# Other planning figures for dealing expert parts over the places of a scan, in a fused scan and mixture-of-experts kernel

## The chip, the cores and the metric

The kernel runs on one core of one Trainium2 chip. Five engines work side by side, each taking its own instructions in order: TensorE (PE in the profile, with its weight loads as PEld), VectorE (DVE), ScalarE (ACT), GpSimd (POOL) and SyncE (SP, which here only issues DMAs). The metric is the device time of one execution in microseconds (us), as the median of several runs. The profile is one further execution, recorded instruction by instruction.

## The reference

The input x is 2 x 2048 tokens of 256 numbers, in float32. It is normalised (layer norm), and two things are added to it:

```
xn  = layernorm(x)
# 1: every token gets a cluster (argmax of cosine with 8 means); tokens are sorted by cluster;
#    over the sorted tokens runs a selective scan, for 256 channels and 16 states each:
h_t = exp(delta_t * A) * h_(t-1) + (delta_t * u_t) * B_t        # per channel and state
y_t = sum over the states of h_t * C_t  +  D * u_t
#    and y is put back in the order of the tokens
# 2: a mixture of experts: 8 experts, each token takes its best 2
h   = silu(xn @ w1[e]) * (xn @ w3[e])                            # 256 -> 512
out = sum over the 2 experts of prob * (h @ w2[e])               # 512 -> 256
x   = x + y + out
```

## The kernel before

**The front** (up to about 100 us) loads x, computes statistics, scores and routes, and lists which tokens go to which expert. After that two streams of work are woven together.

**The scan stream.** The tokens are cut into 8 pieces of 512 (2 batches x 4). Each piece has 8 steps: 4 groups of 4 states, times 2 halves of the channels. So there are 64 steps, and each step has 4 places (one per state), which makes 256 places, numbered 0 to 255 here. At every place VectorE does one multiply (`feed`, L840, for the next place) and one scan (`scan`, L849), and ScalarE makes the decay of the place four further on (`decay`, L834). TensorE works on the step before: at the second place of a step (places 1, 5, 9, ...) it transposes blocks 0 and 1 of the finished states, at the third place blocks 2 and 3 (`Step.turn`, L861), and at the fourth place it contracts them with C (`contract`, L870). ScalarE copies each transposed block out of PSUM (L865); the transposes have two PSUM buffers (`ps_t`), so blocks 2 and 3 need the copies of blocks 0 and 1. In what follows T01, T23 and C stand for these three blocks of TensorE work.

**The expert stream.** Rows are grouped into 71 tiles of 128 rows of one expert; 68 tiles are dealt, the last 3 stand behind a condition at the end. A tile has three parts: up 0 and up 1 (`up`, L954, 16 matmuls each, 256 to 512) and down (`down`, L977, 8 matmuls, 512 to 256). With an up 0 goes a tanh on ScalarE (L962) and a multiply on VectorE (`silu`, L967); with an up 1 the multiply `gate` (L971). These two multiplies are not issued with the part but two places later (`later`, L1044), or when a next part needs them (`vector_work`, L1035). The up parts have one PSUM buffer each. A down part first turns the rows of the tile after next (`turn_tile`, L1059: two transposes L937, a ScalarE copy L939 and two tiny VectorE operations L941, L945), then does its matmuls, a scaling copy on ScalarE (L981), and issues on GpSimd's queue the next rows, the addition to the output (L895) and the next weights (L914). Up 0 of tile 24 is written U0-24 here, its up 1 U1-24, its down D24.

**Who sets the order.** The order of all instructions is written out by a loop at build time (L1159 to L1195) and kept on every engine (`keep_order`). The list `jobs` holds 204 parts in a fixed order: U0-0, U1-0, U0-1, U1-1, D0, U0-2, U1-2, D1, and so on. 7 of them come ahead of the scans; the loop deals the other 197 over the places. Each place has a planned load for TensorE (`on_pe`) and for VectorE (`on_dve`), in us; other work of the pieces is entered with `at_place` (transposes of inputs, projections, step sizes `size`, masks, starting sums `begin`). After each place the loop deals parts as long as the planned TensorE time so far, plus half a part, is under `ratio` times the planned VectorE time so far. `ratio` is planned TensorE time over planned VectorE time of the whole. Before, every part counts 2.05 for TensorE and 0.5 for VectorE:

```
        on_dve[n] += 1.75
            on_pe[n] += (0.0, 0.9, 0.9, 1.1)[n % NSUB]
    PART, PART_DVE = 2.05, 0.5
                pe_now + PART / 2 < ratio * dve_now or place + 1 >= n_places
```

The step sizes of a next piece (`size`, with eight ScalarE operations L732) are held back until the next down part is due (`behind_down`, `size_now`, L1107).

**Within a place** the text order is: feed and scan; T01, T23 or C of the step before; a decay; what `at_place` put there; the parts dealt there; the multiplies that are due.

Of the kernel before, what the change touches and what calls it, by code (L numbers as in the profile page):

```python
# [56 lines left out]
def scan_moe_kernel(  # L57
# [968 lines left out]
    NSUB = Q  # L1026
# [8 lines left out]
    def vector_work(t: int):  # L1035

        for when in sorted(later):
            later[when] = [(u, do) for u, do in later[when] if u > t or do()]

    def part_up(t: int, i: int):  # L1040
        def do():
            vector_work(t - 1)
            tiles[t].up(i)
            later.setdefault(now + 2, []).append((t, tiles[t].silu if i == 0 else tiles[t].gate))  # L1044
            if i == 1 and t + NW < n_dealt:
                tiles[t + NW].load_up()
        return do

    def part_down(t: int):
        def do():  # L1050
            if t + 2 < n_dealt:
                turn_tile(t + 2)
            vector_work(t)
            tiles[t].down()
            if t + NW < n_dealt:
                tiles[t + NW].load_down()
        return do

    def turn_tile(t: int):  # L1059
        tiles[t].turn()  # L1060
        if t + NW < n_dealt:
            tiles[t + NW].load_rows()
# [4 lines left out]
    jobs = []  # L1067
    for t in range(n_dealt + 1):
        if t < n_dealt:
            jobs += [part_up(t, 0), part_up(t, 1)]  # L1070
        if t > 0:
            jobs.append(part_down(t - 1))
    turn_tile(0)
    turn_tile(1)
    p = pieces[0]
# [8 lines left out]
    ahead = len(lead)  # L1084
# [10 lines left out]
    given = ahead  # L1095
    n_places = NSUB * (len(steps) - 1)
# [6 lines left out]
    on_pe, on_dve = [0.0] * n_all, [0.0] * n_all  # L1103
# [3 lines left out]
    def size_now():  # L1107
        while behind_down and (given % 3 == 2 or given == len(jobs)):
            behind_down.pop(0)()
# [39 lines left out]
        at_place(2 * q - 1, 2, lambda q=q: pieces[0].mask_z(q), 0.0, 0.6)  # L1149

    for n in range(NSUB * len(steps)):
        on_dve[n] += 1.75
        if n >= NSUB:
            on_pe[n] += (0.0, 0.9, 0.9, 1.1)[n % NSUB]
    PART, PART_DVE = 2.05, 0.5
    left = len(jobs) - ahead
    ratio = (sum(on_pe[:n_places]) + left * PART) / (sum(on_dve[:n_places]) + left * PART_DVE)
    pe_now = dve_now = 0.0
    for k in range(len(steps)):  # L1159
        step = steps[k]  # L1160
        before_ = steps[k - 1] if k else None
        for i in range(NSUB):
            if i + 1 < NSUB:
                step.feed(i + 1)
            elif k + 1 < len(steps):
                steps[k + 1].feed(0)
            step.scan(i)
            if before_:
                if i == 0:
                    before_.keep_last()  # L1170
                elif i < 3:
                    before_.turn(2 * i - 2)
                    before_.turn(2 * i - 1)
                else:
                    for n in range(JC):
                        before_.contract(n)
            if k + 1 < len(steps):
                steps[k + 1].decay(i)
            for do in plan.pop((k, i), []):
                do()  # L1180
            size_now()
            place = k * NSUB + i
            pe_now += on_pe[place]
            dve_now += on_dve[place]
            while given < len(jobs) and (
                pe_now + PART / 2 < ratio * dve_now or place + 1 >= n_places
            ):
                jobs[given]()
                given += 1
                pe_now += PART  # L1190
                dve_now += PART_DVE
                size_now()
            for _, do in later.pop(now, []):
                do()
            now += 1  # L1195
# [86 lines left out]
```

## Time and profile before

| | us |
|---|---|
| median of 3 runs | 751.91 (751.2 to 751.93) |
| the profiled execution, its own time | 752.28 |
| its span, first to last instruction | 750.5 |
| PE busy | 678.0 |
| PEld busy | 588.9 |
| DVE busy | 678.5 |
| ACT busy | 508.0 |
| POOL busy | 523.0 |
| first scan starts (place 0) | 99.86 |
| last scan ends (place 255) | 735.2 |

The mean granted TensorE clock is 0.951 of full speed, nearly all of the rest in the front. In lines of the timeline the columns are start, duration, engine, source line, operation, what is written and read, count, and in brackets the idle time of the engine just ahead and what ended it. In lines of the waits they are: who waited, at which line, for whom, the total in us, how often, the longest. A matmul's end is modelled in the profile; so the time that a block of matmuls takes on TensorE is read here from its start to the start of the next block.

### The profile page before, as it was taken

To read this page: it belongs to the slowest core of one execution; us is meant where nothing else is said; L and a number is where in the kernel's file an instruction comes from. 1 tells how busy PE (TensorE), PEld (TensorE's weight loads), DVE (VectorE), ACT (ScalarE), POOL (GpSimd) and SP (SyncE) were. 2 spreads that over 40 slices of the span, in tenths; PEclk is the share of its full clock that TensorE was granted. 3 is DMA by queue.
4 is the path that set the end of the run, shared out by engine and by line. 5 is a ranking of instruction groups with operands and counts; after the bars stand their busy time and mean duration, and the time that the engine had idled before them with its cause. 6 is when DMAs were issued, how large, how long until landed. Compare 5 with 4: busy or idle time off the path is not lost.

```text
span 750.5 us, 16877 instructions
## 1 busy us (share of the span) xinstructions
PE 678.0 (90%) x6506; PEld 588.9 (78%) x6506; DVE 678.5 (90%) x1085; ACT 508.0 (68%) x983; POOL 523.0 (70%) x362
## 2 busy tenths in 40 slices
PE   7375779999998999999999999999999998999993
PEld 5144678888877998888878898999798977899982
DVE  8885389899987999999999999999999997999991
ACT  4830446686758866886769577967795768767762
POOL 2023448667777788777877887788788888887733
PEclk9755979999999999999999999999999999999996
DMA  8676544584436755685458656865575547745312
GB/s 269 243 162 233 166 162 92 159 244 138 124 56 171 252 146 117 171 264 148 114 132 281 160 130 124 255 198 132 119 249 157 128 93 219 227 125 118 86 17 29
DMA packets 60401, 120.31 MB, mean 160 GB/s; under 512 B 24160, under 2 KB 41248, under 8 KB 53152
## 3 DMA queue, kind: packets, MB, share of 16 engines
q0 software_dynamic: 38784, 63.71, 36.0%
q1 hardware_dynamic: 21536, 55.50, 21.9%
q8 instruction: 52, 0.85, 0.5%
q14 instruction: 29, 0.24, 0.1%
HBM read 170.78 MB, written 22.28 MB: 257 GB/s over the span
## 4 chain that ended last, share of the span: by engine, by line
PE 69%; ACT 11%; DVE 9%; DMA 5%; issue 4%; POOL 1%; POOLq 0%; ACTq 0%; DVEq 0%
PE p_ps L954 29%; PE py L977 13%; PE pt_s L861 11%; PE y L870 7%; DMA w<-in_w_down_dram,w_row 3%; ACT ht L865 3%; PE y L796 2%; PE pl L342 2%; PE pt_g L937 2%; DMA out_dram<-yo,token_of 2%; ACT da L834 2%; DVE st L374 1%; ACT e L732 1%; ACT r L732 1%; PE px L667 1%
## 5 line engine op out<-in xcount | busy, mean ns | idle before, releaser
L954 PE MATMUL p_ps<-xT,w 128*128 128x128 f32 x2176 | 272.6, 281 | 12.3 <-DVE g L971 8.1
L954 PEld LDWEIGHTS p_ps<-xT,w 128*128 128x128 f32 x2176 | 258.0, 195 | 26.3 <-DVE g L971 8.3
L849 DVE TENSOR_TENSOR_SCAN hs<-da,carry,bu 128x512 f32<-128x512 f32 x192 | 246.0, 1281 | 0.0
L834 ACT ACTIVATE da<-dl,na 128x512 f32<-128x512 f32 x256 | 183.7, 734 | 0.2 <-DVE dl L789 0.2
L840 DVE TENSOR_TENSOR bu<-du,bt 128x512 f32<-128x512 f32 x256 | 173.1, 676 | 0.0
L865 ACT COPY ht<-pt_s 128x512 f32<-128x512 f32 x256 | 138.4, 595 | 40.3 <-PE pt_s L861 39.3
L895 POOL DMA_INDIRECT out_dram<-yo,token_of x68 | 131.4, 1932 | 48.0 <-ACT yo L981 22.6
L914 POOL DMA_INDIRECT w<-in_w_up_dram,w_row x68 | 91.8, 1350 | 89.2 <-DVE w_row L595 43.4
L861 PE MATMUL pt_s<-ident,hs 128*128 128x128 f32 x1024 | 136.8, 277 | 9.7 <-ACT ht L865 8.6
L977 PE MATMUL py<-w,g 128*128 128x256 f32 x544 | 129.8, 381 | 7.5 <-ACT xT L939 4.8
L861 PEld LDWEIGHTS pt_s<-ident,hs 128*128 128x128 f32 x1024 | 116.5, 142 | 21.4 <-ACT ht L865 13.4
L977 PEld LDWEIGHTS py<-w,g 128*128 128x128 f32 x544 | 98.0, 190 | 20.6 <-ACT xT L939 6.0
L928 POOL DMA_INDIRECT xg_sb<-xn,token_of x68 | 91.8, 1349 | 26.2 <-issue 12.8
L914 POOL DMA_INDIRECT w<-in_w_down_dram,w_row x68 | 94.7, 1392 | 20.7 <-issue 13.4
L895 POOL DMA_INDIRECT out_dram<-yt,line_of x32 | 66.1, 2065 | 23.0 <-issue 11.3
L849 DVE TENSOR_TENSOR_SCAN hs<-da,bu 128x512 f32<-128x512 f32 x64 | 78.1, 1221 | 0.0
L962 ACT ACTIVATE t_sb<-p_ps 128x512 f32<-128x512 f32 x68 | 41.0, 603 | 54.5 <-PE p_ps L954 54.4
L870 PE MATMUL y<-ht,z 128*32 128x128 f32 x2048 | 74.0, 277 | 1.5 <-PEq L1208 0.7
L981 ACT ACTIVATE yo<-py,own 128x256 f32<-128x256 f32 x68 | 32.3, 475 | 61.4 <-PE py L977 58.8
L967 DVE SCALAR_TENSOR_TENSOR t_sb<-t_sb,p_ps 128x512 f32<-128x512 f32 x68 | 45.8, 674 | 26.1 <-ACT t_sb L962 26.1
L870 PEld LDWEIGHTS y<-ht,z 128*32 128x32 f32 x2048 | 50.8, 109 | 19.6 <-issue 10.2
L632 POOL DMA_INDIRECT xs<-xn,line_of x32 | 41.8, 1306 | 14.7 <-issue 8.2
(202 smaller groups left out, 582.0 us busy)
## 6 DMA issues: line engine op xcount, KB each, us to landing
bt<-bc SPq DMA_DIRECT2D x31, 1024.0 KB, 5.1
z<-bc SPq DMA_DIRECT2D x32, 256.0 KB, 3.2
xn<-xt SPq DMA_DIRECT2D x8, 520.0 KB, 2.6
xt<-in_x_dram SPq DMA_DIRECT2D x8, 512.0 KB, 8.0
out_dram<-in_x_dram SPq DMA_DIRECT2D x8, 512.0 KB, 8.3
w<-in_w_up_dram,w_row POOLq DMA_INDIRECT x68
w<-in_w_down_dram,w_row POOLq DMA_INDIRECT x68
xg_sb<-xn,token_of POOLq DMA_INDIRECT x68
```

What stands on the lines that cost most here:

```text
L834: nc.scalar.activation(self.da[i], self.piece.dl[:, self.h, :], AF.Exp, scale=na[:, self.h, n : n + 1])
L840: nc.vector.tensor_mul(self.bu[i], self.piece.du[:, self.h, :], self.piece.bts[self.q][:, i, :])
L849: nc.vector.tensor_tensor_scan(self.hs[:, :, i], self.da[i], self.bu[i], start, ALU.mult, ALU.add)
L861: nc.tensor.transpose(pt[:, j, :], self.hs[:, t0 : t0 + G, :].rearrange("p t n -> p (t n)"), ident)
L865: nc.scalar.copy(self.ht[i], pt)
L870: nc.tensor.matmul(p.ys[self.h][j * G : (j + 1) * G, i, :], lhsT=p.zs[q][:, i * (P // G) + j, :], rhs=self.ht[i][:, j, :], start=False, st ...
L895: ins = nc.gpsimd.indirect_dma_start(out=out_rows, out_offset=bass.IndirectOffsetOnAxis(ap=numbers, axis=0), in_=rows, in_offset=None, com ...
L914: nc.gpsimd.indirect_dma_start(out=to[self.t % NW], out_offset=None, in_=rows, in_offset=bass.IndirectOffsetOnAxis(ap=w_row[:, self.t : se ...
L928: nc.gpsimd.indirect_dma_start(out=self.xg, out_offset=None, in_=xn_d, in_offset=bass.IndirectOffsetOnAxis(ap=token_of[:, self.t : self.t ...
L954: nc.tensor.matmul(p[:, f, :], lhsT=wk[:, h, f * P : (f + 1) * P], rhs=self.xT[:, h, :], start=h == 0, stop=h == ND - 1,)
L967: nc.vector.scalar_tensor_tensor(self.s, self.s, 1.0, self.p1, ALU.add, ALU.mult)
L977: nc.tensor.matmul(py, lhsT=self.g[:, f, :], rhs=w2[:, f, :], start=f == 0, stop=f == NH - 1)
```

## The change

The planning figures are replaced, and nothing else: no instruction is added or taken away, and every engine's work is the same.

```diff
--- before.py
+++ after.py
@@ -1070,6 +1070,9 @@
             jobs += [part_up(t, 0), part_up(t, 1)]
         if t > 0:
             jobs.append(part_down(t - 1))
+
+    UP, DOWN, GATE, OWN = 2.0, 2.4, 0.67, 0.36
+    job_pe = [DOWN if n % 3 == 1 and n > 1 else UP for n in range(len(jobs))]
     turn_tile(0)
     turn_tile(1)
     p = pieces[0]
@@ -1149,12 +1152,12 @@
         at_place(2 * q - 1, 2, lambda q=q: pieces[0].mask_z(q), 0.0, 0.6)
 
     for n in range(NSUB * len(steps)):
-        on_dve[n] += 1.75
+        on_dve[n] += 1.95
         if n >= NSUB:
-            on_pe[n] += (0.0, 0.9, 0.9, 1.1)[n % NSUB]
-    PART, PART_DVE = 2.05, 0.5
-    left = len(jobs) - ahead
-    ratio = (sum(on_pe[:n_places]) + left * PART) / (sum(on_dve[:n_places]) + left * PART_DVE)
+            on_pe[n] += (0.0, 1.07, 1.07, 1.14)[n % NSUB]
+    left = sum(job_pe[ahead:])
+    left_dve = (len(jobs) - ahead) * (2 * GATE + OWN) / 3
+    ratio = (sum(on_pe[:n_places]) + left) / (sum(on_dve[:n_places]) + left_dve)
     pe_now = dve_now = 0.0
     for k in range(len(steps)):
         step = steps[k]
@@ -1183,12 +1186,12 @@
             pe_now += on_pe[place]
             dve_now += on_dve[place]
             while given < len(jobs) and (
-                pe_now + PART / 2 < ratio * dve_now or place + 1 >= n_places
+                pe_now + job_pe[given] / 2 < ratio * dve_now or place + 1 >= n_places
             ):
                 jobs[given]()
+                pe_now += job_pe[given]
+                dve_now += (2 * GATE + OWN) / 3
                 given += 1
-                pe_now += PART
-                dve_now += PART_DVE
                 size_now()
             for _, do in later.pop(now, []):
                 do()
```

An up part now counts 2.0 and a down part 2.4 for TensorE; for VectorE each part counts (2 x 0.67 + 0.36) / 3 = 0.57. The scan's own load at each place is entered higher too: VectorE 1.95, TensorE 1.07, 1.07 and 1.14. The sums of the plan become: TensorE 244.7 + 420.4 = 665.1 (before 221.2 + 403.8 = 625.0), VectorE 548.9 + 111.6 = 660.5 (before 498.5 + 98.5 = 597.0), so `ratio` goes from 1.047 to 1.007.

Worked through by the loop's own arithmetic with the one and the other set, 175 of the 197 dealt parts keep their place, and 22 change it, none by more than two places:

| later by one place | later by two | earlier by one |
|---|---|---|
| U0-13 (33 to 34), U1-20 (62 to 63), D27 (95 to 96), U0-30 (101 to 102), U1-35 (122 to 123), D35 (126 to 127), U1-38 (135 to 136), D43 (157 to 158), U0-50 (182 to 183), U0-52 (187 to 188), D51 (188 to 189), D52 (192 to 193), U0-54 (193 to 194), D53 (198 to 199), U0-65 (238 to 239), U0-66 (242 to 243) | U0-46 (162 to 164) | D2 (3 to 2), D4 (10 to 9), U1-16 (52 to 51), U1-18 (57 to 56), U1-40 (145 to 144) |

The order of the parts among themselves stays, and the step sizes of every piece keep their places (14, 48, 80, 111, 142, 174, 208).

## Prediction

> **What bounds the kernel now.** The page first. Both big engines stand at 90%, so shares decide nothing:
>
> ```profile
> PE 678.0 (90%) x6506; PEld 588.9 (78%) x6506; DVE 678.5 (90%) x1085; ACT 508.0 (68%) x983; POOL 523.0 (70%) x362
> ...
> PE 69%; ACT 11%; DVE 9%; DMA 5%; issue 4%; POOL 1%; POOLq 0%; ACTq 0%; DVEq 0%
> ```
>
> The chain that ended last lies on PE for 69%. Who waits for whom settles it. First VectorE's waits from 110 us to the end of the scans, then TensorE's from 110 to 637:
>
> ```profile
> DVE t_sb L967 <- ACT t_sb L962: 18.5, 11, 4.4
> ```
>
> ```profile
> PE pt_s L861 <- ACT ht L865: 8.1, 15, 2.2
> PE py L977 <- ACT xT L939: 4.8, 5, 1.4
> PE p_ps L954 <- ACT xT L939: 2.8, 4, 1.1
> ```
>
> VectorE waits 18.5 us in 11 places, each time for a tanh behind an up 0 that TensorE did late. TensorE's list has no wait for VectorE; it waits for ScalarE copies of its own results. So up to VectorE's last wait TensorE, with ScalarE's copies in it, sets the pace, and VectorE is tied to it again at each wait: places 46 (3.26 us), 52 (4.43), 83 (1.32), 114 (2.05), 177 (0.84), 207 (1.61) and 212, the last:
>
> ```profile
> 631.79 0.16 DVE L945 TENSOR_TENSOR own<-own,xg_sb 128x1 f32<-128x1 f32 x1
> 635.77 0.69 DVE L967 SCALAR_TENSOR_TENSOR t_sb<-t_sb,p_ps 128x512 f32<-128x512 f32 x1 [3.82 <-ACT t_sb L962]
> 636.38 0.68 DVE L840 TENSOR_TENSOR bu<-du,bt 128x512 f32<-128x512 f32 x1
> ```
>
> From 636 VectorE runs without a wait to the last scan (735.2), and 15.3 us of tail follow. The span is therefore: when TensorE reaches U0-57 at place 212 (632.3, tanh done 635.74), plus a stretch set by VectorE. After place 212 only U0-65 and U0-66 move, where their multiplies had 1.0 and 1.15 us to spare; VectorE's operations there stay the same. What counts is how long TensorE takes to get to U0-57.
>
> **What a block costs, by what stands beside it.** The same blocks in TensorE's timeline in two surroundings:
>
> ```profile
> 345.43 2.02 PE L954 MATMUL p_ps<-xT,w 128*128 128x128 f32 x16
> 347.29 1.04 PE L861 MATMUL pt_s<-ident,hs 128*128 128x128 f32 x8
> 348.62 1.15 PE L861 MATMUL pt_s<-ident,hs 128*128 128x128 f32 x8 [0.29 <-ACT ht L865]
> 349.60 1.95 PE L954 MATMUL p_ps<-xT,w 128*128 128x128 f32 x16
> 351.48 1.08 PE L870 MATMUL y<-ht,z 128*32 128x128 f32 x32
> 352.49 0.44 PE L937 MATMUL pt_g<-ident,xg_sb 128*128 128x128 f32 x2
> ```
>
> ```profile
> 504.74 1.04 PE L861 MATMUL pt_s<-ident,hs 128*128 128x128 f32 x8
> 505.71 1.28 PE L870 MATMUL y<-ht,z 128*32 128x128 f32 x32
> 506.92 1.27 PE L954 MATMUL p_ps<-xT,w 128*128 128x128 f32 x9
> ```
>
> Start to start. T01 with T23 right behind takes 347.29 to 348.62, 1.33 (it waits for copies), and that T23 0.98; with a part between each takes 0.87. No part between T01 and T23 costs 0.57. C right behind T23 takes 1.21 (505.71 to 506.92) and T23 before it 0.97; with a part between, C takes 1.01 (351.48 to 352.49), T23 0.87. An up takes 1.79 ahead of a transpose, 1.88 ahead of C or an up; a down 1.73 and 1.82, its two transposes 0.22. So no part between T23 and C costs about 0.3, less 0.1 where the part no longer stands ahead of C. These repeat within 0.1 at most of the 64 steps. A part that moves by a place is one that leaves one of these two gaps or fills it.
>
> **The parts one by one, up to place 212.** Work is equal; only the neighbours change. Sums of block times before and after, us:
>
> - U0-13: T01, up, T23, C 0.87 + 1.79 + 0.97 + 1.21 = 4.84; T01, T23, up, C 1.33 + 0.90 + 1.88 + 1.01 = 5.12 to 5.20: +0.36 at most, taken.
> - U1-18: up, T01, up, T23 1.79 + 0.87 + 1.79 + 0.87 = 5.32; up, up, T01, T23 1.89 + 1.79 + 1.33 + 0.98 = 5.99: +0.67.
> - U1-20: behind C instead of ahead: +0.27. D35 the same with a down: +0.21.
> - U1-40: as U1-18, but T23 had 0.98 before (ScalarE is late behind `size`): +0.41.
> - D43: leaves T01/T23, fills T23/C: +0.36. U0-46: leaves T23/C: +0.31.
> - D51: moves into T01/T23: 1.89 + 0.22 + 1.73 + 1.33 + 0.98 = 6.15 to 1.79 + 0.87 + 0.22 + 1.73 + 0.87 = 5.48: -0.67.
> - D52 and U0-54: each one gap on, so that both are filled: 8.68 to 8.37: -0.31.
> - D53: before, 599.85 (T23) to 606.19 (U0-55) is 6.34, in it a 0.70 wait of its matmuls for a copy and 0.30 for the gathered rows. Behind C and the second input transpose, with the 1.09 that D45 takes in that position: 0.87 + 0.53 + 1.01 + 0.50 + 1.09 + 1.73 = 5.73: -0.61.
> - U0-30 (input transpose and C change sides with it): 6.04 to 6.01. U1-35 (U0-35 still fills its gap), U1-16, D27, U1-38, U0-52, D2 (no TensorE block lies between the two places): 0.
> - U0-50: leaves T23/C, +0.31, but right behind it U0-51 waits 1.09 for a ScalarE copy behind the log and its table loads; the delay falls into that wait: 0. Its tanh now stands behind the log on ScalarE (about 565.1 instead of 561.4), so VectorE's silu at place 184 waits some 0.5, which vanishes in the wait at 207.
> - D4: moves ahead of T23 and saves up to 0.6 of its 1.45 wait, but the listing of rows at place 11 then waits for ScalarE, whose copies of T23 now stand behind the down's scaling copy: bounds -0.3 and +0.2, taken 0, since ScalarE's `num` (done 132.64) ends just before the matmuls that need it (132.75).
>
> Longer: 0.36 + 0.67 + 0.27 + 0.21 + 0.41 + 0.36 + 0.31 = 2.59. Shorter: 0.67 + 0.31 + 0.61 + 0.03 = 1.62. Sum +0.97, say **+1.0 us**, all on the path.
>
> **Queues.** No wait is added by code. On GpSimd D51's loads and addition slip behind the next piece's gather, which brings its rows some 5 us earlier (hence the 0.30 above). Weights are loaded three tiles ahead, about 25 us; no TensorE wait for weights shows, so their issue at another place costs 0. Behind D27 ScalarE has a decay and a sums copy (1.5 us) ahead of the copy for U0-29; it was idle 1.1 us there and the down hides the rest: 0, at most 0.3.
>
> **VectorE.** Where a silu and its gate stand side by side, they take about 0.18 more (place 158: 3.10 against 1.72 for feed and scan plus 1.2). 14 such pairs become 18 (new at 58, 146, 166, 190): 4 x 0.18 = 0.7 us. It is covered by the waits at 83, 177 and 207; without that cover it would be 0.7 on the path.
>
> [...] I take +1.0.
>
> [...] Here a 2.16 us wait was enough once:
>
> ```profile
> 236.00:238.00 2.00, 1.76 (x11) 1.69 (x12) 1.01 (x3) 2.00 (x5) 1.58 (x2) 0.76 0.03 0
> 238.00:240.00 2.00, 2.00 (x12) 2.00 (x11) 0.00 (x0) 1.97 (x4) 1.70 (x2) 0.50 0.84 229
> ...
> 632.00:634.00 2.00, 2.00 (x20) 2.00 (x19) 0.00 (x0) 2.00 (x5) 1.49 (x2) 1.00 0.11 11
> ```
>
> The clock (third number from the end) fell to 0.50 and U0-16 took 3.35 instead of 1.88, 1.47 us on the path; the like wait before 632 left it at 1.00. [...] A slow stretch gone or added is worth 1.5 us either way; I put neither into the forecast.
>
> **How the numbers follow.** The profiled execution took 752.28 (span 750.5 and 1.8 around it), 0.05% above the median of 751.91; 752.28 + 1.0 = 753.3 for such an execution, and carried to the median 751.91 + 1.0 = **752.9 us**. About 0.2%, 1.5 us, is what can be told from no change. The cases:
>
> - **Swaps on TensorE's path**, 752.9: 0.46. Its terms leave about 0.6 either way; same 0.35, slower 0.11.
> - **VectorE hides the swaps, or too few parts move to matter**, 751.9 to 752.6: 0.16, same. For it: the 90%. Against it: no wait of TensorE for VectorE.
> - **Slower: a second slow stretch of the clock** at the 2.16 us wait before U0-57, with nothing left to cover it since VectorE waits right there: 752.9 + 1.5 = 754.4. It decides as soon as the clock shows under 1.00 between 630 and 636. With it, late ScalarE copies behind moved parts that I put at 0: 0.20, slower.
> - **The slow stretch at 236 goes away**: 752.9 - 1.5 = 751.4: 0.05, same.
> - **Faster: only the swaps just ahead of the last waits count.** TensorE catches up on the losses between places 33 and 163, and the 0.67 + 0.31 + 0.61 gained at 188 to 199 stay: 751.9 - 1.6 = 750.3: 0.13. For it: U0-28 and U0-36 start only 0.1 after the silu that frees their buffer, so TensorE is nearly caught up there. Against: VectorE is tied to TensorE at 83 and 114, so both shift together.
>
> Faster 0.13, same 0.56, slower 0.31. The range reaches from the fast rival to the slow one and a little over: 750.3 to 754.9.
>
> **What would show it.** Right: T01 with T23 directly behind at places 33, 57, 145, 157; D51 and D52 between them at 189 and 193; VectorE's waits in the same places, the last still at 212, its silu about 1 us later. Wrong: VectorE's waits gone or the last one elsewhere, TensorE waiting for VectorE, or another clock around 236 or 632.

## The result and the profile after

The changed kernel takes **755.97 us** (median of 11 runs, 755.04 to 762.38). The kernel before, run beside it, takes 752.12 (11 runs, 750.54 to 762.15). The ratio is 1.0074, 95% interval 1.0051 to 1.0097: slower, and above the forecast range. The profiled execution took 755.04, the shortest of the eleven, with a span of 753.2 (before 752.28 and 750.5).

The page, as shown of before:

```profile
PE 677.9 (90%) x6506; PEld 587.9 (78%) x6506; DVE 679.2 (90%) x1085; ACT 508.0 (67%) x983; POOL 517.8 (69%) x362
...
DMA 4%; issue 1%; POOL 1%; POOLq 0%
```

Busy times are nearly the same: VectorE has 0.7 us more, the forecast's four new pairs of multiplies (they stand at places 58, 146, 166 and 190, as forecast). The chain that ended last is now only 6% of the span, followed back along GpSimd's row additions and no further. So the chain has to be left aside, and the stages compared one by one:

| us | before | after |
|---|---|---|
| place 6 starts | 116.47 | 115.37 |
| place 6 to the end of the last scan | 618.70 | 621.21 |
| last scan to the end of the span | 15.32 | 16.64 |

The front differs by 1 to 2 us between executions of the same front: 116.47 before, and in two runs below that change nothing ahead of place 32 about 115.4 (the losses alone) and 114.4 (all gaps filled), worked out from the end of their last scan. What the change did is +2.5 in the scans and +1.3 behind them. The tail of before is itself 0.7 longer than the 14.6 seen in seven of the runs below: its clock fell to half for 3.4 us right behind the last scan, as in the three runs with tails of 14.9 to 15.2, and in none of the seven. So the tail's loss, with the clock left aside, is 2.0.

VectorE's waits (110 to 740 us) and TensorE's (110 to 640):

```profile
DVE t_sb L967 <- ACT t_sb L962: 19.6, 12, 4.4
```

```profile
PE pt_s L861 <- ACT ht L865: 9.0, 18, 2.2
PE py L977 <- ACT xT L939: 4.3, 5, 1.4
PE py L977 <- ACT u L654: 2.5, 3, 1.2
PE p_ps L954 <- ACT xT L939: 2.1, 4, 1.1
...
PE p_ps L954 <- DVE g L971: 1.0, 1, 1.0
```

The last line is new: TensorE waits for VectorE once, which the prediction named as a sign of being wrong. VectorE's last large wait is still at place 212 (0.18 follows at 223):

```profile
636.87 0.69 DVE L967 SCALAR_TENSOR_TENSOR t_sb<-t_sb,p_ps 128x512 f32<-128x512 f32 x1 [4.44 <-ACT t_sb L962]
```

636.87 against 635.77 is +1.1, and +2.2 counted from place 6. Of that 0.6 is the clock: the wait is 4.44 and was 3.82. In these windows the third number from the end is the granted clock; at this wait it was 1.00 before:

```profile
630.00:632.00 2.00, 0.19 (x1) 0.19 (x2) 2.00 (x3) 2.00 (x6) 1.74 (x1) 0.80 0.87 364
632.00:634.00 2.00, 2.00 (x10) 2.00 (x10) 0.40 (x3) 1.58 (x4) 1.65 (x2) 0.50 0.62 68
634.00:636.00 2.00, 2.00 (x19) 1.88 (x22) 0.00 (x0) 1.97 (x4) 1.39 (x3) 0.85 0.39 74
```

The remaining 1.6 is TensorE's list. The forecast had this silu about 1 us later, and +1.1 meets it by luck: a front shorter by 1.1 hides half of the 2.2. The tail is seen in GpSimd's row additions, before and then after:

```profile
726.69 1.56 POOL L895 DMA_INDIRECT out_dram<-yo,token_of  x1 [6.87 <-ACT yo L981]
730.70 1.75 POOL L895 DMA_INDIRECT out_dram<-yo,token_of  x1 [2.45 <-DVE hs L849]
738.41 1.55 POOL L895 DMA_INDIRECT out_dram<-yt,line_of  x1 [5.96 <-ACT yt L808]
```

```profile
728.87 2.57 POOL L895 DMA_INDIRECT out_dram<-yo,token_of  x1 [6.84 <-ACT yo L981]
734.30 2.46 POOL L895 DMA_INDIRECT out_dram<-yo,token_of  x1 [2.86 <-DVE bu L840]
741.14 1.55 POOL L895 DMA_INDIRECT out_dram<-yt,line_of  x1 [4.38 <-ACT yt L808]
```

The first is the addition of D66, the second that of D67, the third the first of the last piece's four. After, D66's issue takes 2.57 instead of 1.56, D67's comes 5.43 behind it instead of 4.01, and the last four start 4.56 after the last scan's end. In seven of the runs below they start 2.53 to 2.55 after it.

### The profile page after: what moved, and what is told of

It reads as the page before. It is cut to its first block, busy times and chain, and to the rows that moved or that the text cites. A ratio compares the mean times of both kernels' runs of the same rounds, so it can differ in the third digit from the quotient of the medians.

```text
span 753.2 us, 16880 instructions
## 1 busy us (share of the span) xinstructions
PE 677.9 (90%) x6506; PEld 587.9 (78%) x6506; DVE 679.2 (90%) x1085; ACT 508.0 (67%) x983; POOL 517.8 (69%) x362
## 5 line engine op out<-in xcount | busy, mean ns | idle before, releaser
L895 POOL DMA_INDIRECT out_dram<-yo,token_of x68 | 136.0, 2000 | 51.2 <-ACT yo L981 22.5
L914 POOL DMA_INDIRECT w<-in_w_up_dram,w_row x68 | 88.1, 1296 | 92.7 <-DVE w_row L595 44.2
L861 PEld LDWEIGHTS pt_s<-ident,hs 128*128 128x128 f32 x1024 | 116.8, 142 | 21.7 <-ACT ht L865 14.6
L928 POOL DMA_INDIRECT xg_sb<-xn,token_of x68 | 88.1, 1295 | 26.2 <-issue 13.4
L895 POOL DMA_INDIRECT out_dram<-yt,line_of x32 | 63.8, 1993 | 24.2 <-issue 12.7
```

The lines of the kernel that those rows point to most:

```text
L861: nc.tensor.transpose(pt[:, j, :], self.hs[:, t0 : t0 + G, :].rearrange("p t n -> p (t n)"), ident)
L895: ins = nc.gpsimd.indirect_dma_start(out=out_rows, out_offset=bass.IndirectOffsetOnAxis(ap=numbers, axis=0), in_=rows, in_offset=None, com ...
L914: nc.gpsimd.indirect_dma_start(out=to[self.t % NW], out_offset=None, in_=rows, in_offset=bass.IndirectOffsetOnAxis(ap=w_row[:, self.t : se ...
L928: nc.gpsimd.indirect_dma_start(out=self.xg, out_offset=None, in_=xn_d, in_offset=bass.IndirectOffsetOnAxis(ap=token_of[:, self.t : self.t ...
```

## The experiments

The kernels take the places from a list: a first pass computes where each part goes by the old figures, single parts are overridden, and the loop deals from that. The job number is 3t - 1 for U0-t, 3t for U1-t, 3t + 4 for Dt, and 203 for D67, the last. The forecast's theory, TensorE's swaps on the path, stands against VectorE binding, against ScalarE's order, and against the tail.

**The gains alone.** Before, with D51, D52, U0-54 and D53 moved:

```diff
+    MOVED = {157: 189, 160: 193, 161: 194, 163: 199}
+    for n, place in MOVED.items():
+        deal[n - ahead] = place
...
-            while given < len(jobs) and (
-                pe_now + PART / 2 < ratio * dve_now or place + 1 >= n_places
-            ):
+            while given < len(jobs) and deal[given - ahead] <= place:
```

> The kernel before with four of the moves alone: D51 to 189, D52 to 193, U0-54 to 194, D53 to 199. Theory 1 (the swaps lie on TensorE's path up to VectorE's last wait at place 212): TensorE reaches U0-57 about 1.4 us earlier (0.67, about 0.2 and 0.5 as the trace after shows), the last scan ends 1.4 us earlier, the time falls to about 750.7. Theory 2 (what was lost came at the very end, in the chain of row additions): within 0.3 us of before, since nothing here touches the end. Theory 3 (the granted clock: the change only brings more slow stretches): the median within 1 us of before, single runs 3 or 7 us longer at a lower mean clock.

Measured 751.81 against 752.08 (ratio 0.9997, 0.9972 to 1.0022): no gain in the time. The trace shows where it went:

```profile
626.00:628.00 2.00, 0.09 (x1) 0.10 (x2) 2.00 (x3) 2.00 (x6) 1.84 (x1) 0.66 0.93 388
628.00:630.00 2.00, 2.00 (x10) 2.00 (x11) 0.50 (x3) 1.58 (x4) 1.55 (x2) 0.50 0.66 72
630.00:632.00 2.00, 2.00 (x11) 2.00 (x11) 0.00 (x0) 1.97 (x4) 1.45 (x2) 0.50 0.42 70
```

Within the wait before U0-57 the clock fell to half for 6.8 us, and VectorE's wait at 212 grew from 3.82 to 5.42. Without that and 0.47 more at place 223, place 6 to the end of the scans is 1.2 shorter than before. The swaps do gain on TensorE; in this execution the clock took it back. One profile can't say how often it does so; that this is what held the median is therefore argued, not shown.

**The losses alone.** Before, with U0-13, U1-18, U1-20, D35, U1-40, D43 and U0-46 moved:

```diff
+    MOVED = {38: 34, 54: 56, 60: 63, 109: 127, 120: 144, 133: 158, 137: 164}
```

> The kernel before with the seven moves that were put down as losses alone: U0-13, U1-18, U1-20, D35, U1-40, D43, U0-46. Theory 1: TensorE is 2.3 us late at place 164 (0.37 + 0.6 + 0.24 + 0.15 + 0.41 + 0.37 + 0.2); some 0.8 of it falls into the wait of U0-51 for a ScalarE copy at place 184, so that the last scan ends 1.5 us later and the time is about 753.6. If nothing is absorbed, 754.4. Theory 2: within 0.3 us of before. Theory 3: median within 1 us of before.

Measured 753.64 (ratio 1.0016, 0.9995 to 1.0037; the medians differ by 1.6). No slow stretch at 212 and a tail of 14.6; place 6 to the end of the scans +2.9. So they cost what they were put at (2.59) or more, and nothing is absorbed in the scans; the forecast's rival that TensorE catches up on the losses falls. That the figures meet is part luck: block by block the seven swaps come to 2.2, and three small delays of 0.23 to 0.28 (at D21, in the contraction ahead of D28, and at D53, whose rows came late) make up the rest. Together with the gains alone (-1.2) this makes +1.7, as much as the changed kernel shows with the clock's share taken off; that too is a coincidence of terms, since the changed kernel lacks two of the three delays and has U0-50 and U0-52 besides.

**U0-52 alone.** Before, with U0-52 at 188:

```diff
+    MOVED = {155: 188}
```

> The kernel before with U0-52 alone one place later (188), where U1-52 follows it in the same place. The prediction put this move at 0. The trace after shows U1-52 waiting 1.0 us for the gate of tile 51, which is now issued at place 188 behind a long VectorE operation: theory 1 with this term gives +1.0 us at U0-53 and about 753.1 in time; without it 752.1. Theory 2: 752.1.

Measured 752.1 (ratio 1.0004, 0.9978 to 1.0030). TensorE's wait for the gate isn't in this trace, although the gate stands behind the 1.20 us multiply here too. TensorE starts U0-52 only 1.13 ahead of that gate (573.40 and 574.53), in the changed kernel 2.28 (576.33 and 578.61). So the move by itself costs nothing; the wait needs TensorE's lead as well, by the order of events from U0-50's move, which brings U0-51 forward; that pair was not run alone.

**The change without its last two moves.** U0-65 and U0-66 stay at 238 and 242:

```diff
-    MOVED = {..., 163: 199, 194: 239, 197: 243}
+    MOVED = {..., 163: 199}
```

> The changed kernel with U0-65 and U0-66 put back to places 238 and 242. The prediction put the two at 0. Theory 2 (the two moves delay D66 and D67 by about 0.5 us and with them the last row additions, which run one behind the other): the tail behind the last scan shortens from 16.6 towards 15.3 us, time 1 us or more under the changed kernel, about 754.5. Theory 1: the last scan ends where it does in the changed kernel (736.6) and the time stays at about 755.6. Theory 3: neither the tail nor the scans change, only the count of slow stretches.

Measured 754.7 (ratio 1.0043, 1.0009 to 1.0076). The tail is 14.6, 2.0 under the changed kernel's, although the scans took 1.6 longer: in this execution U0-57 met 6.8 us of half clock. Four of its 12 executions took 759.8 to 760.5.

**Those two moves alone.** On another chip, where the kernel before took 762.28 (35 runs) with scattered waits; times of that chip are read only as ratios:

```diff
+    MOVED = {194: 239, 197: 243}
```

> The kernel before with U0-65 and U0-66 alone one place later (239, 243). Theory 2 (they delay D66 and D67, and the row additions of the last three tiles and of the last piece run one behind the other): the last scan ends as in before, the tail grows from the 14.6 us that the first four experiments show to about 16.6, the time rises by about 2 us to 754.1. The prediction put these two moves at 0, since their multiplies have over 0.9 us to spare: then the time stays at 752.1.

Ratio 1.0014 (0.9980 to 1.0048). The tail is 14.6: by themselves the two moves don't lengthen it, so "these moves cost 2 us" falls.

**The change without U0-52's move**, same chip:

```diff
-    MOVED = {..., 149: 183, 155: 188, 157: 189, ...}
+    MOVED = {..., 149: 183, 157: 189, ...}
```

> The changed kernel with U0-52 alone put back to place 187. Theory: in the changed kernel U0-50 stands behind the log on ScalarE, its tanh and so VectorE come late, and U1-52, now in one place with U0-52, waits 1.0 us for a gate that is issued behind a long VectorE operation. Without the move the wait goes, TensorE is 1.0 us earlier at U0-53 than in the changed kernel, and the time is 1 us less, about 754.6 to 755. If the wait is covered by something else, the time stays at 755.5 to 756.

Ratio 0.9988 (0.9964 to 1.0011). TensorE's wait for the gate is gone, the tail is 16.3. This chip tells no times apart at 0.3%, and the changed order was not timed beside it; so 1 us from this move is neither shown nor excluded in the time.

**ScalarE's order at the 2.16 us wait.** The places of before; four of the eight step-size operations go one place later, behind the copies of transposed blocks:

```diff
             self.step_size(0)
-            self.step_size(1)
+            half_sized.append(self)
...
+            while half_sized:
+                half_sized.pop(0).step_size(1)
             for do in plan.pop((k, i), []):
```

> The kernel before with the same places for all parts, but the eight ScalarE operations of the step sizes issued as four and four, the second four one place later, behind the copies of the first two transposed blocks. Theory 1 and 3 (TensorE's chain sets VectorE's last wait, and its 2.16 us waits at 236 and 632 bring the slow stretches of the clock): both waits of TensorE shrink to under 1 us, no clock under 1.00 there, VectorE's waits at places 52 and 212 lose 1.4 us each or more, the time falls by 2 to 4 us, to 748 to 750. If VectorE is the bound after all, the time stays at 752.

Ratio 0.9960 (0.9925 to 0.9995). TensorE's wait became 0.70 and 0.87, and neither place 52 nor 212 has a slow stretch. VectorE's wait at 52 fell from 4.43 to 3.63 (the clock's part), not by the 1.4 expected; that at 212 stayed at 3.82, so TensorE's wait for the copies was not what set it, and ScalarE's own work is what is left.

**The same with the gains and U0-50**:

```diff
+    MOVED = {149: 183, 157: 189, 160: 193, 161: 194, 163: 199}
```

> The split step sizes together with the moves that shortened TensorE's chain: D51, D52, U0-54, D53, and U0-50. Theory 1: another 1.3 us (the moves) and 0.5 us (U0-50) off TensorE's way to U0-57, as long as VectorE still waits at place 212; with the split leaving some 2 us of wait there, about 1.5 us under the split alone. If VectorE's wait at 212 is gone with the split, the moves bring nothing more.

Ratio 0.9956 (0.9926 to 0.9986), not told apart from the run before; the 1.5 us expected are not seen in the time.

**The tail.** The changed order again, on another chip:

> The changed kernel's order once more, as the measure for the next run. Theory 1 (the swaps lengthen TensorE's list by some 1.7 us; and the addition of D66 is issued 7.7 us ahead of the end of the scans, runs into an instruction fetch, and holds up the tail by 2.0): about 3.8 us above the kernel before (ratio 1.005), tail 16.3 to 16.7 us, the issue of D66's addition 2.5 us long and the next one 5.4 us or more behind it. Theory 2 (the long tail was an accident of the one profiled execution): tail 14.6, ratio 1.0025.

Measured 755.6 against 752.41 (ratio 1.0054, 1.0031 to 1.0077), tail 16.6, D66's issue 2.56, one slow stretch before U0-57, the wait for the gate 1.0: the first profile repeats. Then both last down parts a place earlier:

```diff
+    MOVED = {..., 197: 243, 202: 248, 203: 250}
```

> The changed order with the last two down parts one place earlier each (D66 249 to 248, D67 251 to 250). Theory 1 (the row addition of D66 must be issued at least some 8 us ahead of the end of the scans, or it falls behind an instruction fetch): D66's addition 8.4 us or more ahead of that end, its issue under 2 us long, the tail 14.6 instead of 16.6, and the time 2 us under the changed order's of the same chip (ratio to before 1.0025). Theory 2 (the tail is set by the last contractions or by the number of additions): tail unchanged at 16.6, no difference between the two. Theory 3 (what is lost lies in more slow stretches of the clock): tail 14.6 but the medians equal.

Measured 760.05 (8 runs; ratio 1.0083, 1.0047 to 1.0120): no better than the 1.0054 of the changed order. The additions behave as theory 1 has it, but TensorE stalls on its own queue (PEq in the profile):

```profile
732.05 1.56 POOL L895 DMA_INDIRECT out_dram<-yo,token_of  x1 [5.97 <-ACT yo L981]
736.09 1.81 POOL L895 DMA_INDIRECT out_dram<-yo,token_of  x1 [2.48 <-DVE hs L849]
...
742.41 0.66 PE L861 MATMUL pt_s<-ident,hs 128*128 128x128 f32 x2 [3.86 <-PEq L1216]
```

D66's issue is short again, the next follows after 4.04, and still the tail is 19.1, because the last transposes stand still for 3.86. What holds PE's queue there was not found. So D66 alone was moved, with everything behind it in its order:

```diff
+    MOVED = {..., 197: 243, 202: 248}
```

> The changed order with D66 alone one place earlier (249 to 248); D67 and everything behind it stay in their order. Theory 1 (the addition of D66 falls behind an instruction fetch): D66's addition is issued 8.5 us or more ahead of the end of the scans, its issue takes under 2 us, the next addition follows 4.0 us later, TensorE has no long stall of its own, the tail is 14.6 to 15.2 and the time 1.4 to 2.0 us under the changed order's (about 754, ratio 1.0025). Theory 2 (the tail is long for another reason): the tail stays at 16.6 although the addition is early.

```profile
739.12 1.56 POOL L895 DMA_INDIRECT out_dram<-yo,token_of  x1 [5.57 <-ACT yo L981]
744.71 1.80 POOL L895 DMA_INDIRECT out_dram<-yo,token_of  x1 [4.03 <-ACT yo L981]
750.64 1.55 POOL L895 DMA_INDIRECT out_dram<-yt,line_of  x1 [4.14 <-ACT yt L808]
```

The tail is 14.6. This ran on a chip where before took 763.07 (ratio 0.9973, 0.9948 to 0.9998). It had no slow stretch before U0-57, which by the table below brings D66 0.4 earlier too, so it isn't the move alone. D67 now came 5.59 behind D66, later than predicted, without harm.

But **my cause, an instruction fetch, does not explain the long issue.** (A fetch is a transfer of 16 KB of the queue that the profile calls `instruction`.) In all these traces the data of D66's addition start 0.56 to 0.58 us after the issue ends, fetch or not. What differs first is the issue itself, and that goes by what VectorE does when it starts. After, and then in the run with only the last two moves:

```profile
728.79 1.28 DVE L849 TENSOR_TENSOR_SCAN hs<-da,carry,bu 128x512 f32<-128x512 f32 x1
```

```profile
737.89 1.80 POOL L895 DMA_INDIRECT out_dram<-yo,token_of  x1 [6.48 <-ACT yo L981]
741.99 2.38 POOL L895 DMA_INDIRECT out_dram<-yo,token_of  x1 [2.29 <-DVE bu L840]
```

After, the issue (728.87) starts 0.08 into a scan. In the other run D66's starts 0.32 into a feed. Before, it starts 0.49 into a gate (726.20) and takes 1.56. The row additions of seven traces (before, the changed order twice, and the first four experiments), grouped by where their issue starts (those of the last piece only in the last row):

| the issue starts | median issue, us |
|---|---|
| under 0.05 into a scan | 1.6 (23 of 34) or 2.6 (11) |
| 0.05 to 0.2 | 2.5 |
| 0.2 to 0.4 | 2.4 |
| 0.4 to 0.6 | 2.1 |
| 0.6 to 0.8 | 2.0 |
| 0.8 to 1.0 | 1.7 |
| over 1.0, up to its end | 1.6 |
| 0.2 to 0.4 into a feed | 1.9 |
| anywhere in a silu or a gate (49 issues) | 1.6, none over 1.62 |
| after the last scan | 1.55 |

The issue takes 1.6 plus what is left of the scan or feed, less some 0.2. Within a silu or a gate, which take 0.67 us as the feed does, it stays at 1.6. That is a correlation over rows, but one with its own control; why a scan or a feed lengthens the issue was not shown, and I made no run that changes either.

**The fetch has a part further on.** One fetch falls near the end of the scans. In the six traces with tails of 16.2 to 16.7 D67's addition lands 1.67 to 3.21 us after its issue ends, and its data end 0.1 to 0.25 behind the end of that fetch. In the other twelve it lands after 1.15 to 1.17, and its data end before that fetch starts. In two of the six D67's issue is short, and the addition is late all the same; the second line is D67:

```profile
736.18 2.56 POOL L895 DMA_INDIRECT out_dram<-yo,token_of  x1 [6.85 <-ACT yo L981]
741.26 1.67 POOL L895 DMA_INDIRECT out_dram<-yo,token_of  x1 [2.52 <-ACT ht L865]
748.52 1.55 POOL L895 DMA_INDIRECT out_dram<-yt,line_of  x1 [5.59 <-ACT yt L808]
```

From before to after D67's landing moves from 1.56 ahead of the last scan's end to 2.18 behind it. Of these 3.74 D66's start is 0.78, the two issues 1.01 and 0.71, the two landings 0.51 and 0.83; the step between the two additions takes 0.09 less. No run moved the fetch, so its share is argued from the order of events.

Which phase D66 meets is set by TensorE's lag. The start of D66's matmuls, counted from the end of the last scan:

| | no slow stretch before U0-57 | with it |
|---|---|---|
| U0-65, U0-66 as before | -11.17, -11.22 | -10.73 to -10.86 |
| moved | -10.76 | -10.38 to -10.40 (changed order, five profiles), -10.42 (without U0-52's move) |

Each is worth 0.4. Either alone puts D66's issue into a feed (tail 14.6, four of four), both put it 0.05 to 0.10 into a scan (16.2 to 16.7, six of six).

**Three more profiles of the changed order**, for the executions of 758.8 to 762.4 that are 4 of its 11 and 2 of 12 in the repeat (before has one such of 11):

> The changed order once more, to see an execution that takes 758 us or more. Theory 1: its extra 3 to 7 us are one long stall of TensorE's own queue in the tail, as in the run with both last down parts moved (3.9 us). Theory 2: they are more slow stretches of the clock in the scans, or scattered waits. If the execution takes 755 to 756, it tells neither.

> As the run before: another profile of the changed order, for an execution of 758 us or more.

> As the run before: another profile of the changed order, for an execution of 758 us or more.

They took 759.8, 762.42 and 768.16, on a chip where before took 763.07. All three have the tail (16.5, 16.7, 16.2) and none a long stall of TensorE's queue. The longest has a further slow stretch at 617 and scattered waits of 0.3 to 1.7. What a chip with such waits shows doesn't explain the long executions on the other two chips; they stay open. Nor do single executions say whether the change costs anything on this chip.

**All gaps filled.** If TensorE binds, a plan that puts a part into nearly every gap of T01, T23 and C should be faster. 44 parts moved by one place; between places 32 and 212 the gaps T01/T23 without a part go from 17 to 0, those T23/C from 19 to 3 (some of the list left out here):

```diff
+    MOVED = {37: 33, 38: 34, 39: 37, 44: 45, 45: 46, ..., 162: 197, 166: 202, 169: 209}
```

> The places of before with 44 parts moved by one place, so that between places 32 and 212 the gaps between T01 and T23 without a part go from 17 to 0, and those between T23 and C from 19 to 3. By the prices of the prediction (0.57 and 0.3 each, less 0.1) TensorE's blocks shrink by 17 x 0.57 + 16 x 0.2 = 13 us. Theory 1 (TensorE's list sets the start of the waits of VectorE at places 83, 177 and 207, but those at 46, 52, 114 and 212 stand on ScalarE's own work and stay): those three waits (1.3, 0.8, 1.6 us) go, TensorE begins to wait for VectorE, and the time falls by 3.3 to 3.8: about 748.5, ratio 0.995. Theory 2 (VectorE binds already and the blocks of TensorE are hidden): no change, ratio 1.000, VectorE's waits the same. Theory 3 (all of TensorE's list is on the path): waits of VectorE at 52 and 212 shrink as well and the time falls by over 6 us, ratio under 0.992.

Measured **748.77** against 752.41 (ratio 0.9945, 0.9922 to 0.9967), with the run behind it the fastest. VectorE's and TensorE's waits:

```profile
DVE t_sb L967 <- ACT t_sb L962: 14.5, 10, 3.2
```

```profile
PE py L977 <- ACT xT L939: 7.9, 6, 1.4
PE pt_s L861 <- ACT ht L865: 3.1, 8, 0.8
```

The size came as theory 1 said, the places didn't. The waits that were to go stayed (83: 1.24; 177's is now 2.23 at 176), only that at 207 nearly went (0.23). Those that were to stand on ScalarE's work shrank: the one at 46 by 1.0, 52 by 1.3, 114 by 2.0, 212 by 0.7, and 1.07 came at 146. Place 6 to the end of the scans is 4.5 shorter, of which some 0.8 is the slow stretch at 52 that is gone (the figure of the run with ScalarE's order). The prices promise 13 us. TensorE's waits for ScalarE's copies of turned rows rose by 3.1 (4.8 to 7.9), while those for copies of transposed blocks, which are part of the prices, fell by 5.0 (8.1 to 3.1); where the rest of the 13 went was not followed. With the step sizes divided as well:

```diff
...
-            self.step_size(1)
+            half_sized.append(self)
...
```

> As the run before, and the last four of the step sizes' eight ScalarE operations one place later, behind the copies of the transposed blocks. Theory 1: in addition no slow stretch of the clock at places 52 and 212 (TensorE's 2.2 us wait there becomes two under 0.9), VectorE's waits there 3.6 and 3.8 instead of 4.2 to 4.4: 0.8 to 1.5 us less than the run before, about 747.5, ratio 0.994. Theory 2 (what binds there is ScalarE's work alone): the same time as the run before within 0.3 us.

Measured 748.63 (ratio 0.9951, 0.9927 to 0.9974): the same, as theory 2 said. The filled order alone already has no slow stretch at 52 and 212, so there was none to remove.

## Why the prediction was wrong

What stood: VectorE's larger waits lie where they were and the last of them is at 212; the four pairs cost 0.7 of busy time; TensorE's swaps are on the path (the losses alone, +2.9 in the scans), and shortening its list shortens the kernel (the filled order, 748.77 against 752.41). Two of the signs named for being wrong came: TensorE waiting for VectorE, and another clock at 632.

**The sum, +1.0, was 1.6.** Block by block (TensorE's start after minus before, counted from place 6):

| step | forecast | measured |
|---|---|---|
| seven losses, with U0-30 and -0.19 by the clock at place 52 taken in | +2.59 | +1.96 |
| D21, not in the forecast: wait for the copy of turned rows 0.72 to 0.99 | 0 | +0.28 |
| U0-50 | 0 | -0.61 |
| U0-52 | 0 | +1.12 |
| D51 | -0.67 | -0.46 |
| D52, U0-54 | -0.31 | -0.20 |
| D53 | -0.61 | -0.51 |
| sum (forecast with U0-30's -0.03) | +0.97 | +1.58 |

The swaps' prices were right in kind and 20 to 55% too large (the seven losses by themselves measure 2.2). The failed terms are the two put at 0. *"U0-50: leaves T23/C, +0.31, but right behind it U0-51 waits 1.09 for a ScalarE copy behind the log and its table loads; the delay falls into that wait: 0"*: the tanh left the front of the log on ScalarE, so the copy for U0-51 came sooner relative to TensorE and its wait fell from 1.09 to 0.33. U0-52, in the list of those with *"(no TensorE block lies between the two places): 0"*: with U0-52 at 188 the gate of tile 51 goes behind the 1.20 us multiply of that place, and U1-52, whose PSUM buffer it frees, waits once TensorE is early enough (U0-52 alone cost nothing):

```profile
579.34 2.05 PE L954 MATMUL p_ps<-xT,w 128*128 128x128 f32 x16 [0.96 <-DVE g L971]
```

```profile
577.49 1.20 DVE L757 TENSOR_TENSOR du<-dl,u 128x1024 f32<-128x1024 f32 x1
578.61 0.68 DVE L971 SCALAR_TENSOR_TENSOR g<-t_sb,p_ps 128x512 f32<-128x512 f32 x1
```

I had checked TensorE's neighbours of U0-52 and not what VectorE does at the place where its buffer-freeing multiply now falls.

**The tail, put at 0, was +2.0.** The step that failed is *"After place 212 only U0-65 and U0-66 move, where their multiplies had 1.0 and 1.15 us to spare; VectorE's operations there stay the same"*, with the tail taken as a fixed 15.3. VectorE's operations did stay the same. But the moves also push D65 to D67 by 0.4, and GpSimd's additions behind them are a chain of their own: D66's issue, its landing, D67's issue, its landing, then the last piece's four. With the clock's 0.4 on top D66's issue fell to the beginning of a scan and took 2.57 instead of 1.56, and D67 landed 3.74 later. Nothing in the forecast followed this chain.

**The clock** was a rival at 0.20 and 1.5 us. It came, for 0.6 at place 212 and 0.2 at 223 in the changed kernel, and it is what added the second 0.4 to D66's lag. With 1.6, 0.8 and 2.0 the profiled parts make 4.4; the medians differ by 3.85 here and 3.2 in the repeat, so 0.5 to 1.2 us of this is not in the usual execution. One profile of before can't say whether its usual tail is 14.6 or 15.3, which is 0.7 of it.

## What to carry to other kernels

When a part moves, follow it on every engine: what stands beside it on the bound engine, what its buffer-freeing operation now stands behind, and whose DMAs are issued after it, down to the last one of the kernel. A tail isn't a constant if a chain of dependent DMAs runs into it from the loop (here 14.6 to 16.7 us). And where a block's cost depends on its neighbours, planning by neighbours (a part in each gap) gave 0.5%, where better averages in the planner lost as much.

## What the hardware showed that I had not expected

- GpSimd's issue of a row addition took longer when it started within one of VectorE's scans or feeds: a median of 2.5 us from 0.05 to 0.2 into a scan and 1.9 from 0.2 to 0.4 into a feed, against 1.55 after the last scan and at most 1.62 in the 49 cases that start in a silu or gate.
- With a TensorE wait of about 2.15 us the granted clock fell to 0.50 in 23 of 28 cases. 14 traces (before, after and the runs that leave ScalarE's order and the gaps as they were) have that wait at places 52 and 212, 28 in all: 5 brought no slow stretch, 17 one of 3.41 us, 6 one of 6.83. The six are those in which the clock fell 0.80 to 1.37 us into the wait, the 17 those in which it fell 1.51 or more after the wait's start; which came looks like chance. In the four runs whose wait there is cut to 1.12 or less none came.
- With D66 and D67 both a place earlier TensorE's own queue stopped for 3.86 us near the end, with no wait for another engine shown; with D66 alone it did not.
- The same kernel took 752.1 and 752.4 us on two chips and 762.3 and 763.1 on others.
